# Attention and quantised FFN on one core: weights of the last projection queued behind a row fetch, a fixed order of evacuation, cast and store, and gate tiles taken one by one

## The chip, the cores and the metric

The kernel runs on one core of a Trainium2 chip. A core has a matrix engine (TensorE, PE in the profile, with its weight loads shown apart as PEld), a vector engine (VectorE, DVE), an activation engine (ScalarE, ACT), GpSimd (POOL) and a sync engine (SyncE, SP). In this kernel SP issues nearly all transfers between the chip's main memory and the on-chip buffers; POOL issues a few. Each engine works through its own list of instructions in order, and semaphores make one engine wait for another or for a transfer. The metric is the device time of one execution in microseconds. A smaller number is better.

## The reference

`x` is 2 batches x 2048 rows x 512 features in float32. Two blocks with residuals are computed:

```python
def xattn(h, ctx):                       # ctx: 128 rows per batch
    q = h @ Wq;  k, v = split(ctx @ Wkv)
    return softmax(q @ k.T / sqrt(512)) @ v

def ffn(x):                              # 512 -> 1536 -> 512
    x    = act_qdq(x)                    # 16-bit: scale = max|x| over the WHOLE tensor / 32767
    up   = act_qdq(x @ w4(w_up).T)       # w4: 4-bit weights in blocks of 32
    gate = act_qdq(x @ w4(w_gate).T)
    sig  = round(sigmoid(gate) * 65536) / 65536
    gate = act_qdq(gate * sig)
    o    = act_qdq(gate * up)
    return o @ w4(w_down).T

x = x + xattn(layernorm(x), ctx)
x = x + ffn(layernorm(x))
```

What shapes the kernel is `act_qdq`: its scale is a maximum over the whole tensor. No row of a tensor can be rounded until all rows of it are known, so each of gate, up and down is a stage that must end before the next one can begin.

## The kernel before

**Stages.** Attention comes first (to 177 us). It leaves the normalised rows in `hT`. Then three FFN stages follow. The 4096 rows are 8 groups of 512 (`TG`), and the 1536 FFN features are 12 blocks of 128, taken as 3 tiles of 4 blocks (`NK` x `NQ`). Integers of 16 bits are split into parts[...] (`split_integers`, lines 229 to 239), so that each product takes 12 matmuls of 128x512: 8 for the sum `q` and 4 for the correction `e` (`project`, lines 512 to 521).

- *Gate* (177 to 457 us): per group and block the `project`, then ACT copies `q` (line 565) and DVE subtracts `e` (line 566). The result goes to memory as `gate_d`. Lines 531 to 538 make the integers `hi` and the first group's parts before it.
- *Up* (457 to 729 us), lines 688 to 742: 24 tiles (`order`, from the last group to group 0), each in two halves `c` = 0 to 47 of 24 matmuls. ACT empties `q` (line 712) and DVE subtracts `e` (line 713). The PSUM pools of `q` and `e` have two buffers of one half each (line 583), so PE can begin half c only when half c-2 has been emptied. On the side, `next_gelu` (lines 632 to 638) reads one gate tile back and has ACT make its integers, its sigmoid and the rounded sigmoid (lines 606 to 608, three passes over 128x2048); DVE then makes the product's integers `pi` (line 644). It is called at c = 0 (three times over c = 0 and 1) and then at each even c. `bound` (lines 650 to 654) keeps for each half the largest |u|·p in a column of `pumax`.
- *The hinge between up and down* (729 to 750 us): the scale of `o` needs the largest product |u|·p in rounded numbers. `fetch_best` (lines 659 to 677) finds for each partition the half with the largest bound, and POOL fetches those rows back from memory with two indirect transfers (line 670, from `up_d` and `p_d`). They are rounded (line 764) and multiplied (line 766), a maximum over the partitions is taken (line 771), and it is compared with a floor. A flag (line 897) is read by all engines (line 899), and a branch that is not taken here covers the case that the bound was not enough.
- *Down* (750 to 1021 us), lines 953 to 974: 32 units `m` of 128 rows. ACT rounds u to `ui` (`round_up`, line 816, for a tile of 256 rows), DVE multiplies it with p to `oi` (line 835) and splits it: `sa` (836), ACT's cast to part 0 (838), part 1 (839), part 2 (843). PE makes `first_sum` (24 matmuls into `yq`, line 851) and `second_sum` (12 into `ye`, line 859). `finish` (lines 862 to 869) has ACT evacuate `yq` (865), POOL add the residual (867), DVE add `ye` (868), and SP store the rows (869). The parts have two buffers, and `yq` and `ye` four each.

**Weights of down.** `load_down` (lines 679 to 685) loads 12 blocks with 3 parts each; a whole block is 768 KB, parts 0 and 1 of it are 512 KB, part 2 is 256 KB. Blocks 0 to 3 (`first_wd`) go into the parts buffer that group 1 leaves, at the start of group 0; blocks 4 to 7 (their parts 0 and 1) after tile 21 and blocks 8 to 11 after tile 22; the part 2 of blocks 4 to 11 after the last store of u:

```python
        in_order(stored, *load_down(range(NE, NF), slice(2, 3)))
```

**What sets the order.** A scheduler of the language lays out each engine's list from the program; `in_order` (lines 158 to 166) forces an order between named instructions, without a wait. SP's transfers are issued in the order of its list and take turns on eight semaphores, so that each waits for the landing of the one eight before it.

Of the kernel before, what the change touches and what calls it, by code (L numbers as in the profile page):

```python
# [49 lines left out]
F32 = mybir.dt.float32  # L50
# [3 lines left out]
I16 = mybir.dt.int16  # L54
# [22 lines left out]
def tile_xattn_ffn(  # L77
# [167 lines left out]
    with ExitStack() as c0:  # L245
# [277 lines left out]
        with ExitStack() as c2:  # L523
# [6 lines left out]
            for c in range(ND):  # L530
                nc.vector.tensor_scalar(hi[:, c, :TG], hT[:, c, :TG], r_h, QMAX, ALU.mult, ALU.min)
            first = split_integers(wk1, homes[0], hi[:, :, :TG], [ND, TG], "g0", ND)
            for t in range(1, NG):
                if t % 2:
                    nc.vector.tensor_scalar(hi[:, :, ts(t, TG)], hT[:, :, ts(t, TG)], r_h, QMAX, ALU.mult, ALU.min)
                else:
                    nc.scalar.activation(hi[:, :, ts(t, TG)], hT[:, :, ts(t, TG)], AF.Copy, scale=r_h)
# [41 lines left out]
    with ExitStack() as c3:  # L579
# [108 lines left out]
        for j, (t, k) in enumerate(order):  # L688
            if k == 0:
                parts = groups.pop(t)  # L690
                if t + 1 < NG and t > 0:
                    groups[t - 1] = load_group(t - 1)
                if t == 0:
                    first_wd = homes[1].tile([P, 3, ND, TG], F32R, tag="parts", name="first_wd")
                    first_wd = first_wd.rearrange("p s c (k d) -> p (s c k d)", k=1).rearrange(
                        "p (f s d) -> p f s d", f=NE, s=3
                    )
                    load_down(range(NE))
            u4 = keep.tile([P, NQ, TG], F32, tag="u4", name=f"u4_{j}")
# [3 lines left out]
            for h in range(2):  # L703
# [22 lines left out]
                if c == 0:  # L726
                    pi = integers_of_p(0)
                if c < 2:
                    next_gelu()
# [8 lines left out]
            else:  # L738
                abs_max(umax[:, j : j + 1], u4[:, :2, :], AX.XY)
            if t == 0 and k + 1 < NK:  # L740
                load_down(range(NE + NQ * k, NE + NQ * (k + 1)), slice(0, 2))
        in_order(stored, *load_down(range(NE, NF), slice(2, 3)))

# [30 lines left out]
    with ExitStack() as c5:  # L774
# [4 lines left out]

        NS = TG // TD  # L780
        groups = [0, *reversed(range(1, NG))]

# [29 lines left out]

        def round_up(t, tiles, places=()):
            ui = wki.tile([P, NF, TD], I16, tag="ui5", name=f"ui5_{t}")
            for k in range(NK):
                made = nc.scalar.activation(  # L816
                    ui[:, ts(k, NQ), :], tiles[k][:, :, ts(t % NS, TD)], AF.Copy, scale=r_u
                )
                in_order(*places[k : k + 1], made)
            return ui  # L820

# [10 lines left out]
        def round_o(parts, pi, ui, c=slice(None)):  # L832
# [4 lines left out]
            ]  # L837
            nc.scalar.copy(parts[0][:, c], sa[:, c])  # L838
            made.append(nc.vector.scalar_tensor_tensor(parts[1][:, c], sa[:, c], -BASE, oi[:, c], ALU.mult, ALU.add))  # L839
            return made  # L840

# [19 lines left out]

        def finish(t, j, q, e, x1):
            m = t * (TD // P) + j
            qs = wk2.tile([P, D], F32, tag="qs", name=f"yqs_{m}")
            nc.scalar.activation(qs, q, AF.Copy, scale=q_o)  # L865
            qx = wk2.tile([P, D], F32, tag="qx", name=f"qx_{m}")
            nc.gpsimd.tensor_tensor(qx, qs, x1[:, j, :], ALU.add)  # L867
            nc.vector.scalar_tensor_tensor(qx, e, e_o, qx, ALU.mult, ALU.add)  # L868
            nc.sync.dma_start(out=of[ds(groups[t // NS] * TG + t % NS * TD + j * P, P), :], in_=qx)

# [18 lines left out]
        tiles_u, kept_p = kept_u[-NK:], kept_p[-NK:]  # L889

        uis = {0: round_up(0, tiles_u, rounded)}
        scale_of_pu()
# [56 lines left out]
        ld = c5.enter_context(tc.tile_pool(name="ld", bufs=2))  # L949
        units = range(TD // P)  # L950
        pieces = [ts(k, NQ) for k in range(NK)]
        p5, x1s = {}, {0: load_x1(0)}
        for t in range(NT // TD):
            if t + 1 < NT // TD:
                x1s[t + 1] = load_x1(t + 1)
                if t + 1 >= NS:
                    p5[t + 1] = load_p(t + 1)
            ui, x1 = uis.pop(t), x1s.pop(t)
            for j in units:
                m, w = t * len(units) + j, ts(j, P)  # L960
                parts = o_parts[m % 2]
                if t < NS:
                    at = ds(t * TD + j * P, P)
                    made = [round_o(parts, kept_p[k][:, :, at], ui[:, c, w], c) for k, c in enumerate(pieces)]
                    in_order(*chain(*made), *[third_part(parts, c) for c in pieces])
                else:
                    round_o(parts, p5[t][:, :, w], ui[:, :, w])
                    third_part(parts)
                q, e = first_sum(m, parts), second_sum(m, parts)
                if j == 0 and t + 1 < NT // TD:  # L970
                    uis[t + 1] = round_up(t + 1, tiles_u)
                    if t % NS == NS - 2 and t + NS < NT // TD:
                        tiles_u = load_up(groups[t // NS + 1])
                finish(t, j, q, e, x1)

# [22 lines left out]
```

## Time and profile before

Three runs took 1026.8, 1028.59 and 1028.76 us; the median is 1028.59 us. The profiled execution took 1027.3 us, of which 1025.5 us are the span from the first to the last instruction.

| stage | from, us | to, us | what the profile has there |
| --- | --- | --- | --- |
| attention, weights of gate | 0 | 177.5 | PE often idle |
| gate | 177.5 | 456.4 | PE without a gap |
| up | 457.3 | 729.1 | PE idle 3.6 us at 478.0 and 0.9 us at 491.7 |
| hinge | 729.1 | 750.2 | PE idle, but for one transpose of 0.29 us |
| down | 750.2 | 1021.4 | PE without a gap over 0.2 us |
| end | 1021.4 | 1025.5 | last addition and store |

Over the span PE is busy for 956.5 us (93%), DVE for 805.1, ACT for 546.5, POOL for 70.2. A line of the timeline gives start and duration in us, engine, source line, operation, output `<-` inputs, shapes, how many (`x`), and in brackets the engine's idle time before it with what ended it. A line of the waits gives who waited for whom, the sum in us, how often, and the longest. The busy digits of the page are tenths of 40 equal slices of 25.6 us.

### The profile page before, as it was taken

How to read it: one execution, taken by the hardware profiler on the slowest of the kernel's cores; microseconds unless marked ns; L12 is line 12 of the kernel's file. 1: busy time of each engine (PE TensorE's matmuls, PEld its weight loads, DVE VectorE, ACT ScalarE, POOL GpSimd, SP SyncE). 2: the span in 40 equal slices, each digit the busy share in tenths (PEclk: the TensorE clock that was granted, in tenths of full speed). 3: DMA queues.
4: the chain of work that ended last, by engine and by line, in shares of the span. 5: the costliest groups of instructions: out<-in, count | busy, mean ns of one | idle time of the engine just before them, and what ended most of it. 6: DMA issues, size and time to landing. Idle time of an engine off the chain costs nothing. (4 is left out here: it accounts for less than half of the span.)

```text
span 1025.5 us, 11691 instructions
## 1 busy us (share of the span) xinstructions
PE 956.5 (93%) x4321; PEld 762.0 (74%) x4321; DVE 805.1 (79%) x996; ACT 546.5 (53%) x647; POOL 70.2 (7%) x67
## 2 busy tenths in 40 slices
PE   6997875999999999998999999999479999999998
PEld 5765743788888878876788888888357888887776
DVE  4579865999997989445898987887589877777775
ACT  2268787332333323219998897887265343434332
POOL 0101111000000000000000000000011211111111
PEclk9999896999999999999999999999879999999999
DMA  9087644887895765896888987896957655754621
GB/s 338 32 313 268 238 186 175 337 334 274 309 384 183 300 226 174 272 395 264 329 326 351 367 318 298 321 387 255 380 210 238 201 151 207 237 201 136 225 84 62
DMA packets 103020, 263.72 MB, mean 257 GB/s; under 512 B 6000, under 2 KB 45936, under 8 KB 94256
## 3 DMA queue, kind: packets, MB, share of 16 engines
q1 hardware_dynamic: 101920, 259.02, 68.8%
q0 software_dynamic: 512, 2.88, 0.8%
q10 hardware_dynamic: 528, 1.05, 0.3%
q8 instruction: 34, 0.56, 0.2%
q14 instruction: 26, 0.21, 0.1%
HBM read 136.05 MB, written 126.88 MB: 256 GB/s over the span
## 5 line engine op out<-in xcount | busy, mean ns | idle before, releaser
L517 PE MATMUL q_g<-parts_g,wg 128*128 128x512 f32 x768 | 195.8, 395 | 5.0 <-ACT parts_g L236 5.0
L517 PEld LDWEIGHTS q_g<-parts_g,wg 128*128 128x128 f32 x768 | 143.5, 188 | 39.0 <-ACT parts_g L236 6.2
L565 ACT ACTIVATE g<-q_g 128x512 f32<-128x512 f32 x96 | 57.3, 599 | 183.0 <-PE q_g L517 176.5
L517 PE MATMUL q_u<-parts_u,wu 128*128 128x512 f32 x576 | 144.2, 392 | 0.0
L517 PEld LDWEIGHTS q_u<-parts_u,wu 128*128 128x128 f32 x576 | 107.9, 187 | 24.6
L851 PE MATMUL yq<-wd,o_parts 128*128 128x512 f32 x512 | 122.2, 391 | 0.0
L851 PEld LDWEIGHTS yq<-wd,o_parts 128*128 128x128 f32 x512 | 96.4, 188 | 21.3
L521 PE MATMUL e_g<-parts_g,wg 128*128 128x512 f32 x384 | 106.1, 395 | 0.0
L566 DVE CUSTOM_DVE_ANT_0 g<-g,e_g 128x512 f32<-128x512 f32 x96 | 64.6, 679 | 38.8 <-PE e_g L521 38.3
L838 ACT CAST o_parts<-sa 128x1536 fp32r<-128x1536 int16 (+1 forms) x40 | 48.6, 1215 | 85.0 <-DVE sa L836 85.0
L816 ACT ACTIVATE ui<-u,r_u 128x1024 int16<-128x1024 f32 x48 | 53.3, 1142 | 68.2 <-DVE oi L835 66.5
L851 PE MATMUL yq<-first_wd,o_parts 128*128 128x512 f32 x256 | 68.7, 410 | 19.5 <-ACT o_parts L838 19.5
L521 PEld LDWEIGHTS e_g<-parts_g,wg 128*128 128x128 f32 x384 | 71.9, 188 | 15.9
L521 PE MATMUL e_u<-parts_u,wu 128*128 128x512 f32 x288 | 77.9, 391 | 0.0
L851 PEld LDWEIGHTS yq<-first_wd,o_parts 128*128 128x128 f32 x256 | 47.9, 192 | 35.6 <-ACT o_parts L838 24.4
L653 DVE CUSTOM_DVE_ANT_0 ua<-ua,pi 128x1024 f32<-128x1024 f32 x47 | 57.4, 1221 | 20.8 <-ACT ua L652 20.6
L644 DVE SCALAR_TENSOR_TENSOR pi<-gi,k_p,sq 128x2048 int16<-128x2048 int16 x24 | 56.3, 2350 | 16.2 <-ACT sq L608 16.2
L713 DVE TENSOR_TENSOR u<-u,e_u 128x1024 f32<-128x1024 f32 x47 | 57.0, 1216 | 8.9 <-ACT u L712 8.8
L859 PE MATMUL ye<-wd,o_parts 128*128 128x512 f32 x256 | 63.9, 391 | 0.0
L521 PEld LDWEIGHTS e_u<-parts_u,wu 128*128 128x128 f32 x288 | 54.0, 187 | 12.3
L868 DVE SCALAR_TENSOR_TENSOR qx<-ye,e_o,qx 128x512 f32<-128x512 f32 x32 | 24.0, 749 | 47.8 <-POOL qx L867 43.3
L839 DVE SCALAR_TENSOR_TENSOR o_parts<-sa,oi 128x1536 fp32r<-128x1536 int16 (+1 forms) x40 | 57.5, 1439 | 3.6 <-DVE sa L836 0.5
(184 smaller groups left out, 1547.5 us busy)
## 6 DMA issues: line engine op xcount, KB each, us to landing
gate_d<-g SPq DMA_DIRECT2D x24, 1024.0 KB, 6.6
up_d<-u SPq DMA_DIRECT2D x48, 512.0 KB, 6.5
gt<-gate_d SPq DMA_DIRECT2D x22, 1024.0 KB, 8.4
u<-up_d SPq DMA_DIRECT2D x21, 1024.0 KB, 8.6
parts_d<-parts_g SPq DMA_DIRECT2D x6, 3072.0 KB, 11.2
parts_u<-parts_d SPq DMA_DIRECT2D x6, 3072.0 KB, 12.2
p_d<-pi SPq DMA_DIRECT2D x24, 512.0 KB, 10.2
p<-p_d SPq DMA_DIRECT2D x84, 128.0 KB, 3.0
```

Source lines behind the costliest of these rows:

```text
L517: nc.tensor.matmul(q, lhsT=w[:, s, c, :], rhs=parts[:, s, c, :], start=(c + s == 0), stop=(c + s == ND))
L521: nc.tensor.matmul(e, lhsT=w[:, 2, c, :], rhs=parts[:, 2, c, :], start=(c == 0), stop=(c == ND - 1))
L565: nc.scalar.activation(g4[:, i, :], q, AF.Copy, scale=1.0 + 1.0 / BASE)
L566: nc.vector.tensor_tensor_reduce(g4[:, i, :], g4[:, i, :], e, 1.0, LOWEST, ALU.subtract, ALU.max, gtop[:, m : m + 1])
L644: nc.vector.scalar_tensor_tensor(pi, gi, k_p, sq, ALU.mult, ALU.mult)
L653: nc.vector.tensor_tensor_reduce(ua, ua, pi, 1.0, 0.0, ALU.mult, ALU.max, pumax[:, c : c + 1])
L713: nc.vector.tensor_tensor(u4[:, both, :], u4[:, both, :], e, ALU.subtract)
L816: made = nc.scalar.activation(ui[:, ts(k, NQ), :], tiles[k][:, :, ts(t % NS, TD)], AF.Copy, scale=r_u)
L838: nc.scalar.copy(parts[0][:, c], sa[:, c])
L839: made.append(nc.vector.scalar_tensor_tensor(parts[1][:, c], sa[:, c], -BASE, oi[:, c], ALU.mult, ALU.add))
L851: nc.tensor.matmul(q, lhsT=parts[s][:, f, :], rhs=wd[f][:, s, :], start=(f + s == 0), stop=(f + s == NF))
L859: nc.tensor.matmul(e, lhsT=parts[2][:, f, :], rhs=wd[f][:, 2, :], start=(f == 0), stop=(f == NF - 1))
```

## The change

1. *Table.* A sigmoid of one column is put at the start of gate, on ACT, so that the load of the sigmoid's table stands there and no longer in front of the first sigmoid of up.
2. *Gate tiles.* `next_gelu` is called once at c = 0, once at c = 1, once at each even c from 2, and once more at c = 13. Before, c = 0 and 1 had three calls.
3. *Weights of down.* Blocks 0 to 3 come without their part 2 at first. Blocks 4 to 7, parts 0 and 1, come after tile 21 as before. The part 2 of blocks 0 to 3 comes after tile 22, where blocks 8 to 11 stood. Blocks 8 to 11 (parts 0 and 1) and the part 2 of blocks 4 to 11, twelve loads of 4 MB in all, come after the last store of u; before, these were eight loads of 2 MB.
4. *Down.* For group 0, `ui` is rounded for one unit of 128 rows at a time. The first unit's first tile is cut in two pieces. `finish` becomes `finish_first` (evacuation by ACT and addition by POOL) and `finish` (addition of `ye` by DVE and store), both two units later. Forced orders: on ACT the evacuation of unit m-2 before the first cast of unit m, and the rounding of the next u after the last cast of m; on DVE the addition of unit m-2 after the last part of m.

```diff
             first = split_integers(wk1, homes[0], hi[:, :, :TG], [ND, TG], "g0", ND)
+            table = const.tile([P, 1], F32, name="table")
+            nc.scalar.activation(table, unit, AF.Sigmoid)
...
-                    load_down(range(NE))
+                    load_down(range(NE), slice(0, 2))
...
-                if c < 2:
+                if c in (1, NH // 4 + 1):
                     next_gelu()
...
-            if t == 0 and k + 1 < NK:
-                load_down(range(NE + NQ * k, NE + NQ * (k + 1)), slice(0, 2))
-        in_order(stored, *load_down(range(NE, NF), slice(2, 3)))
+            if t == 0 and k == 0:
+                load_down(range(NE, NE + NQ), slice(0, 2))
+            if t == 0 and k == 1:
+                load_down(range(NE), slice(2, 3))
+
+        rest = load_down(range(NE + NQ, NF), slice(0, 2)) + load_down(range(NE, NF), slice(2, 3))
+        in_order(stored, *rest)
...
+        def round_up(ui, tiles, t, at=0, width=TD):
+            return [
+                nc.scalar.activation(
+                    ui[:, ts(k, NQ), ds(at, width)],
+                    tiles[k][:, :, ds(t % NS * TD + at, width)],
+                    AF.Copy,
+                    scale=r_u,
+                )
+                for k in range(NK)
+            ]
...
+        def finish_first(m, q, x1):
             qs = wk2.tile([P, D], F32, tag="qs", name=f"yqs_{m}")
-            nc.scalar.activation(qs, q, AF.Copy, scale=q_o)
+            made = nc.scalar.activation(qs, q, AF.Copy, scale=q_o)
             qx = wk2.tile([P, D], F32, tag="qx", name=f"qx_{m}")
-            nc.gpsimd.tensor_tensor(qx, qs, x1[:, j, :], ALU.add)
-            nc.vector.scalar_tensor_tensor(qx, e, e_o, qx, ALU.mult, ALU.add)
+            nc.gpsimd.tensor_tensor(qx, qs, x1[:, m % NU, :], ALU.add)
+            return made, qx
+
+        def finish(m, qx, e):
+            made = nc.vector.scalar_tensor_tensor(qx, e, e_o, qx, ALU.mult, ALU.add)
...
-        uis = {0: round_up(0, tiles_u, rounded)}
+        uis = {0: up_integers(0)}
+        in_order(rounded[0], *round_up(uis[0], tiles_u, 0, 0, P))
...
+        for m in range((last + 1) * NU + 2):
+            if m - 2 in sums:
+                q, e = sums.pop(m - 2)
+                t = (m - 2) // NU
+                evacuated, qx = finish_first(m - 2, q, x1s[t])
...
+                    sizes = [2, 2, NQ, NQ] if m == 0 else [NQ] * NK
...
+                if m > 1:
+                    in_order(evacuated, casts[0])
+                sums[m] = first_sum(m, parts), second_sum(m, parts)
+                if m + 1 < NS * NU:
+                    t, j = divmod(m + 1, NU)
+                    if j == 0:
+                        uis[t] = up_integers(t)
+                    in_order(casts[-1], *round_up(uis[t], tiles_u, t, j * P, P))
+                    if m + 2 == NS * NU:
+                        tiles_u = load_up(groups[1])
+                elif t < last and j == (NU - 1 if t + 1 == NS else 0):
+                    uis[t + 1] = up_integers(t + 1)
+                    in_order(casts[-1], *round_up(uis[t + 1], tiles_u, t + 1))
...
+            if m > 1:
+                stored = finish(m - 2, qx, e)
+                if m - 2 < last * NU + NU - 2:
+                    in_order(made[-1], stored)
```

## The prediction

> **What bounds the kernel.** I read the page first, its busy slices, to see where PE is not full.
>
> ```profile
> PE   6997875999999999998999999999479999999998
> PEclk9999896999999999999999999999879999999999
> ```
>
> From slice 7 on PE is full but for slice 18 (461 to 487 us) and slices 28 and 29 (718 to 769). Matmuls are not changed, so time can come only from there. The waits of PE in 440 to 720 us and from 720 on name the two places:
>
> ```profile
> PE q_u L517 <- ACT u L712: 4.6, 2, 3.6
> PE yq L851 <- ACT o_parts L838: 19.5, 5, 18.8
> ```
>
> The timeline at the start of up shows the first:
>
> ```profile
> 464.82 3.90 ACT L606 ACTIVATE gi<-gt,r_g 128x2048 int16<-128x2048 f32 x2 [0.63 <-DMA wu<-wu_d]
> 468.62 3.88 ACT L607 ACTIVATE gt<-gi,s_g 128x2048 f32<-128x2048 int16 x2
> 472.41 3.69 ACT L608 ACTIVATE sq<-gt 128x2048 uint16<-128x2048 f32 x2
> 476.95 1.91 ACT L712 ACTIVATE u<-q_u 128x1024 f32<-128x1024 f32 x2
> 478.01 5.10 PE L517 MATMUL q_u<-parts_g,wu 128*128 128x512 f32 x15 [3.62 <-ACT u L712]
> ```
>
> Two gate tiles go through ACT in pairs, 11.5 us, ahead of the evacuation of half 1 that PE needs for half 3. The next windows show what the stall also costs: the granted clock is 0.50 in 478 to 481 us, so 3.0 us of matmuls do 1.5 us of work.
>
> The timeline of the hinge shows the second:
>
> ```profile
> 725.04 5.40 SPq L723 DMA_DIRECT2D up_d<-u  x2
> ...
> 728.01 0.16 DVE L665 SCALAR_TENSOR_TENSOR row<-where,lane 128x1 uint32<-128x1 uint32 x1
> ...
> 730.50 6.02 SPq L684 DMA_DIRECT2D wd<-wd_d  x8
> ...
> 736.21 1.07 POOL L670 DMA_INDIRECT best<-up_d,row  x1 [275.90 <-DMA wd<-wd_d]
> ...
> 742.72 1.15 ACT L764 ACTIVATE ui_b<-best,r_u 128x1024 int16<-128x1024 f32 x1 [9.30 <-DMA best<-up_d,row]
> ...
> 745.17 4.49 ACT L816 ACTIVATE ui<-u,r_u 128x1024 int16<-128x1024 f32 x4 [1.30 <-DVE two L766]
> ...
> 747.86 0.75 DVE L835 SCALAR_TENSOR_TENSOR oi<-pi,k_o,ui 128x512 int16<-128x512 int16 x1 [1.17 <-DVEq L900]
> ...
> 749.57 0.60 ACT L838 CAST o_parts<-sa 128x512 fp32r<-128x512 int16 x1
> ...
> 750.22 3.78 PE L851 MATMUL yq<-first_wd,o_parts 128*128 128x512 f32 x8 [18.76 <-ACT o_parts L838]
> ```
>
> The row is known at 728.17, yet POOL fetches only at 736.21. The fetch reads `up_d`, so it needs the store of half 46, issued at 725.04; that one transfer took 10.2 us to land by the trace (735.3), and POOL starts 0.9 later. The page gives 6.5 us as this kind of store's median. The windows say why it is slow: the DMA share is 0.98 to 1.05 in every stretch from 705 to 740. About 400 GB/s move without a pause, and the store stands behind `wd` loads.
>
> [...] the fetch landed after 6.5 us while SP's eight loads were under way. [...]
>
> **The change part by part.**
>
> *Table.* 1.28 us leave ACT at 461.6 and come, with about 0.3 us of sigmoid, in front of an `hi` of 2.0 us and the group's casts 3 and 4, which end at 180.94 and would end near 182.5. By the built order, PE then has four matmuls of block 1, and further corrections, ahead of those casts' matmuls: twelve matmuls by about 182.0, the other twelve of the two blocks at 0.23 us each from 182.1, about 185.0. Before, block 1 ends at 185.2 (the last four start at 184.13). I take 0. At worst the whole 1.6 us shows; it cannot gain.
>
> *Gate tiles.* Replay ACT in its built order with the rows' durations: maxima from 461.3 (0.8 without the table), u of half 0 to 463.3, gi 1.98, `ua` 1.05, sigmoid 1.98, then u of half 1 from 468.4 to 469.4. PE arrives at half 3 at 474.4, five us later. Next sq 1.88, gi, `ua`, sigmoid, u of half 2 to 477.3; PE arrives at half 4 at 479.8. Both stalls go: 3.62 + 0.93 + the 1.5 of the clock = 6.1 us. What is late next: ACT has 2x1.0 (u) + 2x1.05 (`ua`) + 1.98 + 1.98 + 1.88 = 9.9 us per tile against 11.1 us of PE. The added call at c = 13 puts 5.8 us into a slack of 1.2 per tile, so about five tiles run with evacuations late; half-deep buffers cover most of it, and following the list I find some 1 us of PE waits between halves 13 and 24. Gain 5, between 3 (stalls of 3 there) and 6.1. Gate tile loads need no earlier landing: two are on chip at 463.5, and SP's issues are only spread out.
>
> *Weights of down.* Ahead of the store of half 46 stand 1 MB of part 2 less (four loads of 512 KB, not 768) and then 1 MB where 2 MB stood. At 410 KB per us that is 2 MB / 0.41 = 5 us. The backlog is then gone by about 728.5, and the store lands by 729.4 (5.9 earlier; the floor is 2.6 us, which the lightly loaded store at 693.46 needed, or 727.7, but the row is not ready before 728.2). Fetch at 730.0 for 736.2: 6.2 us gained, between 5 and 7.2. The price: SP now issues twelve loads from 730.5, each 0.5 to 0.75 us and never over eight in flight, to about 739. Queued behind them on SP are the flag and the x1 loads, not needed before the flag at 740. Their 4 MB need 10 us, to about 742, beside the fetch. The fetch had 2 MB in flight beside it before, so its 6.5 us may stay; I allow 0 to 2 more and take 0.5. Block 8 is wanted six us after PE's start and lands by 735; part 2 is wanted later still. All of this is relative to PE's end of up, so it adds to the other gain.
>
> *First unit of down.* From DVE's first `oi` to PE's first matmul: 2.36 us (747.86 to 750.22), as four roundings of 1.14 hold ACT until 749.66. In the changed order three half-size roundings (about 0.6 each) stand there, and the first piece has 256 elements, not 512: 0.4 + 0.2 + 0.35 + 0.3 for signals = 1.25. Gain 1.1. The next pieces come at 1.05 and 1.75 us; PE, at half clock for its first 3.8 us, takes 1.9 per piece, so it does not run dry.
>
> *Order in down.* From 750 to 1021 PE has four gaps of 0.17 to 0.19 us: at most 0.7 to gain. Per unit DVE needs 1.82 + 0.56 + 1.76 + 1.75 + 0.75 = 6.6 us and ACT 1.47 + 0.68 + 1.5x1.14 = 3.9, in PE's 8.44. The evacuation of m-2 is old when the cast of m comes, so the forced order waits for nothing. The tight place is unit 4. By the built order its cast follows the evacuation of unit 3, which ends its first sum 2.77 us before unit 4 begins: 0.68 + 1.47 = 2.15 leaves 0.6, if `ui` is there. Its u loads are now issued after x1 (that waits for POOL's addition of unit 1) and land near 29 us after PE's start; `ui` ends at 30.2, `sa` at 32.7, the cast at 35.3, PE wants it at 35.8. I take +0.7 to -1.5, and 0.4 gained.
>
> *Sum.* 0 + 5.0 + 6.2 - 0.5 + 1.1 + 0.4 = 12.2 us. The profiled execution goes from 1027.3 (span 1025.5) to 1015.1. The median lies 1.3 above that execution, so 1016.4.
>
> **Rivals.** (A) The fetch is not sooner: POOL starts at 730, but 4 MB of SP's loads hold it until their end near 742, plus 2. The attribution "DMA wd" in POOL's line speaks for a tie to the loads; the 6.5 us beside a full queue speaks against. Then the hinge gains only 0.1, and 5 + 0.1 + 0.4 leave about 1023. (B) The stall moves: with only one tile of lead ACT falls behind, and up loses at halves 13 to 24 what it won at 3 to 5. For it: ACT is busy 175 of the 200 us from 500 to 700. Then 7.2 are left: about 1021. (C) Slower: in down the three roundings of the next `ui` (3.4 us) come to stand between an evacuation and the next cast. After a first sum's end 2.77 us are left, 0.68 + 3.42 + 1.47 = 5.6 are needed: 2.8 us per 256 rows, fourteen times, 39 us: about 1055. It decides from 0.9 us per 256 rows, where 12.2 are eaten. Against it: the built order has evacuation, cast, evacuation, cast, and only then the roundings.
>
> **How the numbers follow.** A difference of 0.2% (2 us) is what a measurement of this kernel can tell. Likeliest, with its own range of 1012.5 to 1019: 0.62. (A) 0.13, (B) 0.13, both at once, near 1028, 0.05, (C) 0.07. Faster 0.62 + 0.13 + 0.13 = 0.88, same 0.05, slower 0.07. From 1011.5 to 1022.5 the range holds the likeliest, most of (B) and half of (A): 0.8.
>
> **What would show it.** Right: no wait of PE for u over 1 us near 478 and clock 1.00 there; POOL's fetch within 2 us of the row, about 6 us after half 46's store is issued or sooner; PE idle for about 13 us, not 19, before its first `yq`; 36 matmuls per 8.44 us after that. Wrong: ACT of the fetched u more than 8 us after POOL's start (A); PE waits for u past 520 us (B); PE waits for casts in every second unit, or at unit 4 (C); a wait at 180 us (table). The forecast fails if the backlog ahead of half 46 is set by something other than the 2 MB removed.

## The result, and the profile after

The changed kernel takes 1022.36 us (median of five runs, 1020.75 to 1023.37) where the kernel before takes 1028.67 (five runs beside it). The ratio is 0.9932, with a 95% interval of 0.9913 to 0.995. The gain is 6.3 us: about half of the 12.2 that were forecast. It lies just inside the whole range given (1011.5 to 1022.5 us), and outside the range that the likeliest outcome had for itself (1012.5 to 1019). Where it was made and lost is quite different from the forecast, and that is the subject of what follows.

The busy slices of the changed kernel's page, from the same rows as before:

```profile
PE   6998874999999999999999999999488999999998
PEclk9999997999999999999999999999789999999999
```

The dip at slice 18 (461 to 487 us) is gone from the row of PE; the row of the clock has a 9 there before and after. The dip of the hinge (slices 28 and 29) is still there, and slice 30 has a small new one in the row of PE. The waits of PE, for 440 to 720 us and for 720 us on (who waited for whom, sum in us, times, longest), say the same:

```profile
PE q_u L517 <- ACT u L715: 0.3, 1, 0.3
...
PE yq L865 <- ACT o_parts L854: 20.4, 2, 17.1
```

The wait of up has fallen from 4.6 us to 0.3. The wait for `o_parts` was 19.5 with a longest of 18.8. It is now larger in sum, with a longest of 17.1: there is a second one, of 3.23 us, inside down. The timeline at the start of up and in the hinge:

```profile
463.92 2.00 ACT L609 ACTIVATE gi<-gt,r_g 128x2048 int16<-128x2048 f32 x1 [0.99 <-DMA wu<-wu_d]
...
468.67 1.00 ACT L715 ACTIVATE u<-q_u 128x1024 f32<-128x1024 f32 x1
...
476.70 2.03 PE L517 MATMUL q_u<-parts_g,wu 128*128 128x512 f32 x8
...
720.62 4.18 SPq L726 DMA_DIRECT2D up_d<-u  x2
...
723.08 0.16 DVE L668 SCALAR_TENSOR_TENSOR row<-where,lane 128x1 uint32<-128x1 uint32 x1
...
724.90 10.40 SPq L687 DMA_DIRECT2D wd<-wd_d  x12
...
729.99 1.07 POOL L673 DMA_INDIRECT best<-up_d,row  x1 [270.09 <-DMA wd<-wd_d]
...
737.00 1.15 ACT L772 ACTIVATE ui_b<-best,r_u 128x1024 int16<-128x1024 f32 x1 [8.75 <-DMA best<-up_d,row]
...
743.43 3.78 PE L865 MATMUL yq<-first_wd,o_parts 128*128 128x512 f32 x8 [17.14 <-ACT o_parts L854]
```

One gate tile, not two, stands ahead of the evacuation at 468.67, and no matmul waits. In the hinge the row is known at 723.24 but POOL fetches at 729.99, 6.75 us later. Before, it was 8.04. The store of half 46, issued at 720.62, needed 8.4 us to land by the trace (before: 10.2). That is the step where the forecast had expected 6.2 us and got about one.

The new wait in down, at the fifth unit of 128 rows (unit 4), in the timeline of the changed kernel:

```profile
764.80 1.60 SPq L801 DMA_DIRECT2D u<-up_d  x3
...
775.12 1.15 ACT L828 ACTIVATE ui<-u,r_u 128x1024 int16<-128x1024 f32 x1 [1.04 <-DMA u<-up_d]
...
775.91 4.02 POOL L880 TENSOR_TENSOR qx<-yqs,x 128x512 f32<-128x512 f32 x2 [14.41 <-DMA out<-qx]
...
776.31 2.51 DVE L850 SCALAR_TENSOR_TENSOR oi<-p,k_o,ui 128x1536 int16<-128x1536 int16 x1 [1.76 <-ACT ui L828]
...
778.85 1.50 DVE L851 TENSOR_SCALAR sa<-oi 128x1536 int16<-128x1536 int16 x1
...
781.96 3.60 PE L865 MATMUL yq<-first_wd,o_parts 128*128 128x512 f32 x8 [3.23 <-ACT o_parts L854]
```

ACT waits for the third of the three loads of u. DVE then needs 2.51 and 1.50 us for two operations that took 1.82 and 0.56 in the kernel before, while POOL makes two additions. PE stands for 3.23 us, and the granted clock is 0.50 for the next 3.4 us.

The two profiled executions, stage by stage (times from the first and last matmul of each stage):

| stage | before, us | after, us | gained |
| --- | --- | --- | --- |
| up to the first matmul of up | 457.32 | 456.92 | 0.4 |
| up | 271.73 | 266.60 | 5.1 |
| hinge: PE's last `q_u` or `e_u` to its first `yq` | 21.18 | 19.91 | 1.3 |
| down | 271.19 | 272.11 | -0.9 |
| end | 4.12 | 3.87 | 0.2 |
| span | 1025.5 | 1019.4 | 6.1 |

The 0.4 us of the first row are no gain of the change: in the other kernels below, up begins between 456.1 and 458.6 us.

### The profile page after: what moved, and what is told of

It is laid out like the page before. It is cut to its first block, busy times and chain, and to the rows that moved or that the text cites. A ratio compares the mean times of both kernels' runs of the same rounds, so it can differ in the third digit from the quotient of the medians.

```text
span 1019.4 us, 11685 instructions
## 1 busy us (share of the span) xinstructions
PE 953.6 (94%) x4321; PEld 764.6 (75%) x4321; DVE 806.2 (79%) x1000; ACT 549.4 (54%) x655; POOL 90.4 (9%) x67
## 3 DMA queue, kind: packets, MB, share of 16 engines
q0 software_dynamic: 512, 2.88, 0.7%
q10 hardware_dynamic: 528, 1.05, 0.3%
## 5 line engine op out<-in xcount | busy, mean ns | idle before, releaser
L865 PEld LDWEIGHTS yq<-wd,o_parts 128*128 128x128 f32 x512 | 96.6, 189 | 21.1
L865 PE MATMUL yq<-first_wd,o_parts 128*128 128x512 f32 x256 | 68.3, 411 | 20.4 <-ACT o_parts L854 20.4
L878 ACT ACTIVATE yqs<-yq,q_o 128x512 f32<-128x512 f32 x32 | 22.0, 687 | 119.1 <-PE yq L865 119.1
L880 POOL TENSOR_TENSOR qx<-yqs,x 128x512 f32<-128x512 f32 x32 | 64.5, 2016 | 210.6 <-ACT yqs L878 152.0
L865 PEld LDWEIGHTS yq<-first_wd,o_parts 128*128 128x128 f32 x256 | 50.1, 196 | 32.7 <-ACT o_parts L854 21.0
L857 DVE SCALAR_TENSOR_TENSOR o_parts<-sa,oi 128x1536 fp32r<-128x1536 int16 (+2 forms) x41 | 58.2, 1438 | 19.9 <-PE ye L873 19.9
L656 DVE CUSTOM_DVE_ANT_0 ua<-ua,pi 128x1024 f32<-128x1024 f32 x47 | 57.1, 1220 | 18.8 <-ACT ua L655 18.6
L853 DVE SCALAR_TENSOR_TENSOR o_parts<-sa,oi 128x1536 fp32r<-128x1536 int16 (+2 forms) x41 | 58.6, 1430 | 14.9 <-PE yq L865 13.0
L854 ACT CAST o_parts<-sa 128x1536 fp32r<-128x1536 int16 (+2 forms) x41 | 48.8, 1190 | 34.4 <-DVE sa L851 34.4
## 6 DMA issues: line engine op xcount, KB each, us to landing
parts_d<-parts_g SPq DMA_DIRECT2D x6, 3072.0 KB, 11.1
```

What stands on the lines that cost most here:

```text
L656: nc.vector.tensor_tensor_reduce(ua, ua, pi, 1.0, 0.0, ALU.mult, ALU.max, pumax[:, c : c + 1])
L857: return nc.vector.scalar_tensor_tensor(parts[2][:, c], sa[:, c], BASE + 1.0, oi[:, c], ALU.mult, ALU.subtract)
L865: nc.tensor.matmul(q, lhsT=parts[s][:, f, :], rhs=wd[f][:, s, :], start=(f + s == 0), stop=(f + s == NF))
L880: nc.gpsimd.tensor_tensor(qx, qs, x1[:, m % NU, :], ALU.add)
```

## The experiments

Three questions came out of this comparison, and the theories carry these names in the expectations:

- *Where did the gain of the hinge go?* T1: the gate-tile edit leaves ACT's last gate tiles later relative to PE, the store of half 43 comes late, and the weight loads that SP has queued behind it restore the backlog. T2: the backlog ahead of half 46 never depended on the 2 MB. T4: the fetch itself is slowed by the loads that run beside it. T5: its duration is its own.
- *What makes the wait at unit 4?* T3: the late loads of u. Its rival: the collision of POOL and DVE.
- *What is the forced order in down worth?* T6: the order is what counts. T7: it is enough that the evacuations and additions come two units later.

All times below are medians. Ratios are to the kernel before, run on the same chip beside them. The stage figures are of each kernel's profiled execution.

| kernel | time, us | ratio, 95% interval | up | fetch issued / p rows landed, after PE's end of up | hinge | units 3 and 4 together | twelve units 19 to 30 |
| --- | --- | --- | --- | --- | --- | --- | --- |
| before | 1028.67 | | 271.7 | 7.2 / 14.3 | 21.2 | 17.0 | 103.0 |
| changed | 1022.36 | 0.9932 (0.9913 to 0.995) | 266.6 | 6.5 / 14.5 | 19.9 | 21.5 | 99.4 |
| gate tiles alone | 1021.22 | 0.9925 (0.9907 to 0.9943) | 266.4 | 6.0 / 13.7 | 20.7 | 16.6 | 102.9 |
| weights of down alone | 1027.41 | 0.9992 (0.9982 to 1.0002) | 272.4 | 3.6 / 13.0 | 21.6 | 16.6 | 101.9 |
| down alone | 1029.29 | 1.0007 (0.9998 to 1.0016) | 272.7 | 7.3 / 14.6 | 20.4 | 22.4 | 99.4 |
| changed, old gate tiles | 1027.48 | 0.9996 (0.9985 to 1.0006) | 273.1 | 3.7 / 12.7 | 18.2 | 22.4 | 99.4 |
| changed, no early table | 1018.81 | 0.9909 (0.9895 to 0.9924) | 266.2 | 2.6 / 12.0 | 17.4 | 24.2 | 99.4 |
| changed, loads ahead of the store | 1020.51 | 0.9917 (0.9901 to 0.9933) | 269.2 | 1.9 / 11.4 | 16.8 | 23.9 | 99.4 |
| changed, rest behind the flag | 1023.28 | 0.9945 (0.9932 to 0.9958) | 268.4 | 6.1 / 11.8 | 17.2 | 24.6 | 99.4 |
| changed, tile rounded whole | 1018.47 | 0.9901 (0.9889 to 0.9914) | 267.2 | 6.3 / 14.4 | 19.8 | 18.1 | 99.4 |
| changed, three qx buffers | 1022.77 | 0.9942 (0.9929 to 0.9955) | 267.2 | 5.9 / 14.6 | 20.0 | 21.1 | 99.4 |
| changed, two orders not forced | 1021.96 | 0.9943 (0.9929 to 0.9956) | 266.6 | 5.6 / 14.4 | 19.7 | 20.9 | 99.4 |
| loads ahead + rounded whole | 1018.19 | 0.9904 (0.9888 to 0.992) | 267.8 | 2.0 / 11.8 | 17.2 | 17.6 | 99.4 |
| the same + part 2 behind the flag | 1017.04 | 0.99 (0.9884 to 0.9915) | 266.6 | 1.8 / 11.1 | 16.5 | 17.9 | 99.4 |

A unit is counted from its first `yq` matmul to that of the next unit, so that the wait of PE for unit 4 falls into unit 3, and the slow clock after it into unit 4.

How far a stage differs by itself can be read from four of these kernels that are alike up to down: the changed one, and those with the tile rounded whole, with three qx buffers and with two orders not forced. Their up is 266.6 to 267.2 us, their fetch is issued 5.6 to 6.5 us after PE's end of up, and their hinge is 19.7 to 20.0.

### The edits one by one

**Gate tiles alone**, in the kernel before:

```diff
-                if c < 2:
+                if c in (1, NH // 4 + 1):
```

> The gate-tile calls alone, in the kernel before. Both theories: up from its first matmul to its last is about 5 us shorter (271.7 before, 266.6 in the changed kernel), since both stalls of PE near 478 and 491 us go. For the hinge (PE's last matmul of up to its first of down, 21.2 us before) they differ. T1 (the last gate tiles come later relative to PE, and with them the store of half 43 and the weight loads queued behind it): the hinge gets longer by 1 to 4 us, and the kernel gains 1 to 4 us in all. T2 (the backlog of transfers ahead of half 46 does not hang on this): the hinge stays at 21.2 and the kernel gains 5 us, about 1023.5.

Up falls by 5.4 us, as both theories said. But the hinge does not get longer; at 20.7 it is 0.5 shorter. T1 in this form falls: this edit by itself delays nothing. It is also faster, by its median, than the whole change. The intervals overlap, so I only say that the other edits together brought nothing that can be measured. The kernel with the old gate tiles, below, says the same from the other side.

**Weights of down alone**, in the kernel before (the third part of the change, nothing else):

```diff
-                    load_down(range(NE))
+                    load_down(range(NE), slice(0, 2))
...
-        in_order(stored, *load_down(range(NE, NF), slice(2, 3)))
+        rest = load_down(range(NE + NQ, NF), slice(0, 2)) + load_down(range(NE, NF), slice(2, 3))
+        in_order(stored, *rest)
```

> The new placing of down's weights alone, in the kernel before. Up stays at 271.7 us. T1 (the gate-tile edit ate the gain of this one): with the gate tiles where they were, the store of half 46 lands within 4 us and the fetch is issued 4 to 6 us earlier relative to PE's end of up than before (7.2 us after it): hinge 15.5 to 17 us instead of 21.2, about 1023.5. T2 (the backlog never hung on the 2 MB that the edit moves away): hinge 20 to 21 us, about 1028.

Neither theory is right. The fetch is issued 3.5 us earlier, so the backlog does hang on the 2 MB (against T2), though not by 5. The fetch then takes 8.3 us to land where it took 6.5, and what is left is lost in the next step. The timeline of this kernel, between the fetch and PE's start:

```profile
742.87 6.34 ACT L820 ACTIVATE ui<-u,r_u 128x1024 int16<-128x1024 f32 x6 [1.33 <-DVE two L770]
...
749.39 1.66 ACT L842 CAST o_parts<-sa 128x512 fp32r<-128x512 int16 x3 [0.17 <-ACTq L904]
```

The scheduler has put six roundings of u in ACT's list ahead of the first cast. The kernel before had four there. An edit of SP's loads has moved ACT's list.

**Down alone**, in the kernel before: everything of the fourth part of the change.

> The new order of down alone, in the kernel before. The hinge is about 1.1 us shorter (first piece of half size). Then T3: a stall of PE of 3 to 5 us at the fifth unit of 128 rows, with its lost clock, is paid, and the last twelve units run at 8.28 us each instead of 8.60, which returns about 4: about 1.5 us in all faster, 1027. If the stall hung on the other edits instead, it is absent here and the gain is 5 to 6 us, 1023.

T3's account holds in its parts. The hinge is 0.8 shorter. The stall at unit 4 is there without the other edits: a wait of 4.1 us, and units 3 and 4 cost 5.4 us more. The late units run at 8.28 us and return 3.6. The first unit takes 0.9 longer. The time was expected at 1027 and came out at 1029.3: within the interval, this edit alone gains nothing.

**The changed kernel with the old gate tiles** (`c < 2` again):

> The changed kernel with the gate-tile calls of the kernel before. Up is 5 us longer, 271.7. T1: the hinge is 4 to 5 us shorter than in the changed kernel (19.9), 15 to 16 us, so the time stays within 1 us of 1022.4. T2: the hinge stays at 19.9 us and the time is 5 us longer, about 1027.4.

The time is 1027.48, as T2 had it. The ratio of 0.9996 has an interval that holds 1: without the gate tiles the three other edits together gain nothing that can be measured. The hinge lies in between: 18.2, not 15 to 16 and not 19.9. Of these 1.7 us, 1.6 are lost again in down (273.8 us instead of 272.1). Compared with down alone (20.4), which differs by the weights and the early table, the placing of the weights is worth 2.15 us here: the fetch is issued 3.6 earlier and takes 8.1 instead of 6.7.

**The changed kernel without the early table:**

```diff
-            table = const.tile([P, 1], F32, name="table")
-            nc.scalar.activation(table, unit, AF.Sigmoid)
```

> The changed kernel without the early sigmoid. If the prediction's nothing for this edit holds: within 1 us of 1022.4. In detail: the load of 1.28 us stands ahead of the first sigmoid of up again, so that ACT's list in the first five halves is 1.3 us later; a delay of 2.2 us there (a late landing of the first gate tile, in another execution) gave a wait of PE of 1.5 us near half 5, so 0.6 us of wait are expected here, and 0 to 0.4 come back at the start of gate: plus 0.5.

I expected half a microsecond more. By the ratios the time fell by about 2.4 us (0.9909 against 0.9932), but the intervals overlap. The trace has the key to the hinge, which is 17.4 us instead of 19.9. The wait near half 5 is there as expected (0.62 us). The cause of the shorter hinge is 20 us ahead of it. ACT's list in the changed kernel, in the timeline, with SP behind it:

```profile
705.06 1.00 ACT L715 ACTIVATE u<-q_u 128x1024 f32<-128x1024 f32 x1
...
709.12 2.21 SPq L687 DMA_DIRECT2D wd<-wd_d  x4
```

and in the kernel without the table:

```profile
702.13 1.03 ACT L713 ACTIVATE u<-q_u 128x1024 f32<-128x1024 f32 x1 [0.42 <-PE q_u L517]
...
704.87 2.28 SPq L685 DMA_DIRECT2D wd<-wd_d  x4
...
727.32 1.07 POOL L671 DMA_INDIRECT best<-up_d,row  x1 [265.78 <-DVE m_u L752]
```

Both first lines are the evacuation of half 43. Without the table it stands ahead of the last gate tile's sigmoid and runs as soon as PE is done. With the table the scheduler has laid the list so that the sigmoid, an absolute value and the rounded sigmoid come first. The store behind it is issued 20.3 us before PE's end of up without the table and 14.8 before it in the changed kernel, 5.5 later. SP works through its list in order, and the four loads of blocks 4 to 7 stand behind that store (issued at 708.70 in the changed kernel). In the changed kernel PE had freed their buffers at 701.5, yet they were issued from 709.12 on, and the DMA share meanwhile (a window of the trace: start:end, length, busy times by engine, clock, DMA share, GB/s) was

```profile
704.00:707.00 3.00, 3.00 (x15) 2.49 (x14) 2.43 (x3) 2.83 (x3) 0.00 (x0) 1.00 0.00 1
```

nothing at all. Two megabytes that could have moved then stood in front of half 46's store later. ACT's list in up is the same in this kernel as in the one with the gate tiles alone, so the difference is the table's. It takes both edits, though: with the old gate tiles, ACT's list in up is that of the kernel before, table or not. T1's chain (late evacuation, late store, loads held behind it, restored backlog) was right; the gate tiles by themselves did not start it.

That these 2.5 us reach the time is not shown. The profiled execution of this kernel was the slowest of its five (1022.9 us; the others 1017.5 to 1020.7). In it units 3 and 4 took 24.2 us instead of 21.5, and hinge and down together 292.5 instead of 292.0.

### The chain of the hinge, taken at two other links

**Loads of blocks 4 to 7 ahead of half 43's store:**

```diff
+                if c == NH - 5:
+                    load_down(range(NE, NE + NQ), slice(0, 2))
                 stored = nc.sync.dma_start(out=up_d[c], in_=u4[:, both, :])
...
-            if t == 0 and k == 0:
-                load_down(range(NE, NE + NQ), slice(0, 2))
```

> The changed kernel, but the loads of blocks 4 to 7 stand on SP ahead of the store of half 43 (which came late from ACT) and no longer behind it. T1 (this queueing gave the fetch's gain away): the loads are issued near 702 instead of 709 us, the pause of the transfers from 705 to 709 is filled, and the fetch is issued 2.5 to 4 us after PE's end of up, where the changed kernel has 6.5 and the one with the old gate tiles 3.7. As the fetch then takes about 8 us beside 4 MB of loads, it lands some 2 earlier and the hinge is 18 us instead of 19.9: about 1020.5. If the late store of half 43 is not the cause: fetch at 6.5, hinge 19.9, 1022.4.

The evacuation is as late as in the changed kernel, but the loads no longer wait for it. The timeline of this kernel:

```profile
703.74 2.20 SPq L687 DMA_DIRECT2D wd<-wd_d  x4
...
727.67 1.07 POOL L673 DMA_INDIRECT best<-up_d,row  x1 [268.16 <-DVE umax L169]
```

The fetch is issued 1.9 us after PE's end of up and the hinge is 16.8, 3.1 less than in the changed kernel. That shows the link from SP's order to the hinge. The time, 1020.5, is as expected, with an interval that overlaps that of the changed kernel. The hinge gave more than the 1.9 us expected, but in the profiled execution up had a wait of 1.5 us near 487 (the first gate tile landed 2.2 us later), and units 3 and 4 cost 2.4 us more.

**The twelve last loads behind the flag:**

```diff
-        rest = load_down(range(NE + NQ, NF), slice(0, 2)) + load_down(range(NE, NF), slice(2, 3))
-        in_order(stored, *rest)
...
         p5, x1s = {}, {0: load_x1(0)}
+        rest = load_down(range(NE + NQ, NF), slice(0, 2)) + load_down(range(NE, NF), slice(2, 3))
+        in_order(x1_loads[0], *rest)
```

> The changed kernel, but the twelve loads of 4 MB that stood behind the last store of u are issued only behind the flag and the first x1 load, so that no load runs beside the fetch. T4 (the fetch is slow because of the loads that run beside it): POOL's fetch is issued at the same point, about 6.5 us after PE's end of up, and lands within 3.5 us instead of 7.0; the hinge is 16 to 16.5 us instead of 19.9 and the time about 1018.5, unless PE then waits for block 8 in its first sum. T5 (6.5 to 7 us are what this fetch costs by itself): the fetch still takes 6.5, the hinge stays within 0.5 us, 1022.

The timeline of this kernel, fetch and first use:

```profile
731.23 1.08 POOL L673 DMA_INDIRECT best<-up_d,row  x1 [271.52 <-DVE two L772]
...
735.65 1.15 ACT L770 ACTIVATE ui_b<-best,r_u 128x1024 int16<-128x1024 f32 x1 [5.81 <-DMA best<-up_d,row]
```

4.4 us from issue to landing with nothing beside it (the 3.5 of the expectation was an estimate), against 7.0 in the changed kernel and 8.1 to 8.3 where the fetch is issued early beside the 4 MB. T4 holds, T5 falls. The hinge is 2.7 us shorter, about what the fetch saved. The gain did not reach the time, which is 1023.3 and not 1018.5. In the profiled execution the first two units, whose matmuls are interleaved on PE in this kernel, took 0.9 us more together, and units 3 and 4 took 3.1 us more, with a wait of PE at unit 4 that grew to 5.1 us.

### Unit 4

**The second tile of group 0 rounded whole**, one unit earlier than its second half would be, so that its buffers come free for the next u:

```diff
-                if m + 1 < NS * NU:
+                if m + 2 < NS * NU:
...
-                    in_order(casts[-1], *round_up(uis[t], tiles_u, t, j * P, P))
-                    if m + 2 == NS * NU:
+                    in_order(casts[-1], *(round_up(uis[t], tiles_u, t, j * P, P) if t == 0 else round_up(uis[t], tiles_u, t)))
+                    if m + 3 == NS * NU:
```

> The changed kernel, but the second tile of group 0 is rounded whole after the first unit's casts of down's unit 1, so that the next group's u is loaded one unit earlier. T3 (the stall at unit 4 comes from the u loads, which wait for the last rounding in halves): the loads are issued near 759 instead of 764.8 us and land by 770; the wait of PE of 3.2 us at unit 4 falls below 0.5, the clock is not halved there, and the time is 4 to 5 us shorter, about 1018. If the collision of POOL's additions with DVE makes the stall, a wait of 1.5 us or more stays, and the gain is 1 to 2.

The timeline of this kernel:

```profile
757.09 2.45 SPq L801 DMA_DIRECT2D u<-up_d  x3
...
776.14 1.82 DVE L850 SCALAR_TENSOR_TENSOR oi<-p,k_o,ui 128x1536 int16<-128x1536 int16 x1 [0.55 <-ACT ui L828]
...
780.17 2.22 PE L865 MATMUL yq<-first_wd,o_parts 128*128 128x512 f32 x8 [1.18 <-ACT o_parts L854]
```

The loads are issued 7.7 us earlier and have all landed by 767.6. The wait of PE is 1.18 us, not below 0.5, but the clock stays at 1.00, and units 3 and 4 cost 18.1 us instead of 21.5. The time is 1018.5, 3.2 us below the changed kernel by the ratios, whose intervals overlap by 0.0001. T3 holds for most of the stall.

The wait at unit 4 also decides what a shorter hinge is worth. It stands in the changed kernel and in six variants of it: old gate tiles, no early table, loads ahead of the store, rest behind the flag, three qx buffers, two orders not forced. In the profiled executions of these seven the hinge goes from 20.0 down to 16.8 us, yet hinge and down together take 291.6 to 293.3 in all of them. The third u lands 50.0 to 51.8 us after PE's end of up, whether down began early or late, so what the hinge saves is mostly spent at unit 4. Why the landing hardly moves was not tried.

**Three buffers for qx:**

```diff
-            qx = wk2.tile([P, D], F32, tag="qx", name=f"qx_{m}")
+            qx = wk2.tile([P, D], F32, tag="qx", name=f"qx_{m}", bufs=3)
```

> The changed kernel with three buffers for qx instead of two: POOL's addition of unit 2 no longer waits for the store of unit 0, which lands late behind the 3 MB of u loads. The multiplication and the split of unit 4 on DVE (2.51 and 1.50 us while POOL adds) fall back to 1.82 and 0.56, the cast comes 1.6 us earlier, and PE's wait at unit 4 falls from 3.2 to about 1.6: 1.5 to 2 us faster than the changed kernel, 1020.6. If POOL's additions do not slow DVE, both durations stay and so does the time.

The multiplication fell back to 1.82 us, but the split did not. The timeline of this kernel at unit 4:

```profile
778.68 2.33 POOL L880 TENSOR_TENSOR qx<-yqs,x 128x512 f32<-128x512 f32 x1 [4.82 <-ACT yqs L878]
...
779.91 1.52 DVE L851 TENSOR_SCALAR sa<-oi 128x1536 int16<-128x1536 int16 x1
```

POOL's addition of unit 2 now waits for its evacuation, which ACT makes only after the late roundings (777.93). So it still falls on unit 4. PE's wait went from 3.23 to 2.60, and the time did not change. The part of the collision that went was worth 0.6 us of PE's wait, and the split still takes 1.0 us more than its 0.56. The collision is itself a consequence of the late u, and a buffer does not remove it.

### The forced order in down

```diff
-                if m > 1:
-                    in_order(evacuated, casts[0])
...
-                stored = finish(m - 2, qx, e)
-                if m - 2 < last * NU + NU - 2:
-                    in_order(made[-1], stored)
+                finish(m - 2, qx, e)
```

> The changed kernel without two of its forced orders in down (evacuation of unit m-2 ahead of the first cast of unit m, addition of unit m-2 behind the last part of unit m); the evacuations and additions still come two units later. T6 (the forced order is what keeps DVE from waiting for POOL's addition in the late units): the unit of 128 rows takes 8.5 us or more again in the last third, and the time is 2 to 4 us longer than the changed kernel, 1024.5 to 1026.5. T7 (coming two units later is enough, the forced order does nothing): the late units stay at 8.28 us, and the time is within 1 us of 1022.4.

The scheduler then puts the cast of unit m ahead of the evacuation of unit m-2 and the addition ahead of the next multiplication, but the late units stay at 8.28 us and the time at 1022. T7 holds and T6 falls. What made the late units slow in the kernel before is in its window of eight of them (start:end, length, busy times of PE, PEld, DVE, ACT and POOL, clock, DMA share, GB/s):

```profile
936.00:1005.00 69.00, 68.47 (x290) 53.52 (x290) 52.44 (x40) 25.86 (x25) 10.39 (x9) 1.00 0.43 142
```

and in its waits of DVE over the same stretch:

```profile
DVE qx L868 <- POOL qx L867: 14.1, 8, 2.0
```

52.4 us of work and 14.1 of waiting for POOL leave DVE 2.5 of 69: there DVE, not PE, sets 8.6 us per unit. PE's weight loads show it: in this stretch they waited 3.4 us for ACT's cast of what DVE had split. In the kernel without the two orders the same wait, over its stretch of eight units, is

```profile
DVE qx L884 <- POOL qx L880: 10.7, 9, 1.2
```

still there, but at most 1.2 us each and inside PE's 8.28. In the changed kernel it is gone from this stretch, and DVE waits for PE. The addition comes two units later, and POOL has mostly done its part.

### Both cures together

Loads ahead of the store and the tile rounded whole:

> The loads of blocks 4 to 7 ahead of the store of half 43 and the second tile of group 0 rounded whole, both in the changed kernel. If the two causes are separate, their gains add: hinge 16.8 us instead of 19.9 (3.1) and a stall at unit 4 of 1.2 us without the loss of the clock (3.3): about 1016. If the earlier start of down only makes PE wait longer at unit 4 (the u loads hang on ACT, whose roundings start when down starts, so it should not): 1018 to 1019.

The same, with the part 2 of blocks 4 to 11 behind the flag:

> As the kernel with both edits, and the part 2 of blocks 4 to 11 (eight loads, 2 MB) is loaded only behind the flag and the first x1 load; blocks 8 to 11, parts 0 and 1, stay ahead of the fetch. T4 says that the fetch takes 8.2 us beside 4 MB and 4.4 beside none, so about 6.5 beside 2 MB: hinge 15 to 15.5 us instead of 16.8, and 1014.5. Part 2 is first wanted some 7 us after PE's start of down and lands about 8 us after the flag; if it comes late, PE waits for it in the first unit and the gain is lost: 1016 or more.

In the traces the gains add: hinge plus down is 286.1 and 285.4 us, against 292.0 in the changed kernel and 288.6 with the tile rounded whole alone. In the times they hardly do: 1018.2 and 1017.0, where 1016 and 1014.5 were expected, with intervals that hold 0.9901, the ratio of the rounded tile alone. That the hinge's 2.5 us reach the time is therefore seen in the trace and not shown by the clock. The last expectation's estimate of the fetch was wrong: beside 2 MB it takes 8.0 us, as beside 4 MB. PE does not wait for part 2. The last kernel has the lowest median of all, 1.0% below the kernel before (0.99, interval 0.9884 to 0.9915). Its interval and that of the changed kernel (0.9913 to 0.995) overlap by 0.0002. It cannot be told apart from the kernel with only the tile rounded whole.

## Why the prediction was right in total and wrong in its parts

The total was right by luck. The forecast was 6.0 us too low, and the measured time is 0.14 us inside the end of a range that had been drawn wide enough for most of (B) and half of (A). It is a time that the prediction gave to these rivals, though (B) did not happen and (A) only in part. By experiment the whole gain, as far as it can be measured, is that of the gate tiles: 0.9925 with them alone, 0.9996 with everything but them. What the weights were to bring did not come, and the gain and the loss in down nearly cancelled. Of the signs that the prediction named for being right, only the one at 478 us and the pace of the units came true. The fetch came 6.75 us after the row and not within 2, PE stood 19.9 us before its first `yq` and not 13, and it waited at unit 4, which had been named as a sign of being wrong.

- **Table: 0 predicted.** The load of the sigmoid's table takes 1.28 us in both traces, at 461.60 in the kernel before (`461.60 1.28 ACT L607 ACT_TABLE_LOAD   x1`) and at 177.25 in the changed one. The prediction is right at the edit's own place: from the first matmul of gate to that of up, all executions here took 279.8 to 280.9 us, with the table or without it. Wrong elsewhere: together with the gate tiles it cost 2.5 us of hinge. I looked for its price where the instruction stands and not at what else the scheduler had laid differently, though ACT's list of up, which the prediction replays for its first halves, has half 43 behind the last sigmoid.
- **Gate tiles: 5.0.** Measured 5.1 in the changed kernel and 5.4 alone. The expected microsecond of waits in halves 13 to 24 was one wait of 0.3. With it the prediction's own terms give 5.8 (6.1 less 0.3); the other 0.7 is not accounted for, and up differs by 0.6 between kernels that are alike there. Rival (B) is out.
- **Weights of down: 6.2 less 0.5.** Beside the old gate tiles and with the new down, 2.15 us of hinge (18.2 against 20.4); in the kernel before and in the changed kernel, nothing. The first failing step is "the backlog is then gone by about 728.5": 2 MB at 410 KB per us should have moved the landing of half 46's store by 5 us, and it moved by 3.5 where nothing else interfered (6.2 to 2.7 us after PE's end). The "About 400 GB/s move without a pause" behind it holds from 715 us on; from 705 to 710 the same windows have 369, and from 710 to 715 they have 333. The trace shows where the time went: with the old gate tiles the store of half 43 lands 3.1 us sooner, but from there to the landing of the last of the next four loads, 2 MB, it takes 7.5 us instead of 5.1. Why it does is open. The second failing step is "I take 0.5" for the slower fetch: it was 1.5 (6.7 to 8.1). So rival (A) was partly true: the loads slow the fetch but do not hold it to their end (in the changed kernel it landed at 736.98 us and the last of them at 742.08). The third is the table. The fourth is "so it adds to the other gain": while the wait at unit 4 stood, what was won in the hinge was lost there. The condition I had named as fatal, that something other than the 2 MB sets the backlog, came true: SP's order behind a late store.
- **First unit of down: 1.1.** Right. From the first `oi` to PE's first matmul it took 1.29 us (742.14 to 743.43) instead of 2.36. That is nearly all of the 1.3 us that the hinge gained. The 0.3 us for signals in the sum were an estimate; the trace has 0.04, 0.08 and 0.06 between the four instructions. The half clock of PE's first 3.8 us is in the windows of both: the granted clock is 0.50 from 733.6 to 754.0 us in the kernel before and from 727.2 to 747.6 in the changed one, and 1.00 behind it.
- **Order in down: 0.4, from +0.7 to -1.5.** The net in down was -0.9, inside that range, but as the difference of two terms that were both missed. The gain in the late units, 3.6 us, was held to at most 0.7, because I counted PE's four visible gaps (0.7 us) and not the pace of the units, which rose from 8.28 to 8.6 without gaps. The loss at unit 4 was about 4.6 us: the third u landed 31.7 us after PE's start and not 29, and the 1.82 and 0.56 us of DVE were taken from a row in which POOL was not adding at that moment. The waits of the kernel before had the sign of the first: DVE waited 43.3 us for POOL's additions from 720 on.

The kernel before shows the collision of POOL and DVE, early in down:

```profile
757.46 0.29 DVE L836 TENSOR_SCALAR sa<-oi 128x512 int16<-128x512 int16 x1
...
759.09 1.29 POOL L867 TENSOR_TENSOR qx<-yqs,x 128x512 f32<-128x512 f32 x1 [13.48 <-ACT yqs L865]
...
759.25 1.28 DVE L836 TENSOR_SCALAR sa<-oi 128x512 int16<-128x512 int16 x1
```

A split of 128x512 took 0.29 us alone and 1.28 when it started 0.16 us after an addition of POOL of 1.29. In the changed kernel it took 1.38 when it started 0.06 us after one (760.27). At 798.76 there, DVE's multiplication started 0.07 us ahead of an addition: it kept its 1.80 us, and the addition took 2.88. What makes the two engines hold each other up, no run here shows. The prediction should have priced it.

## What to carry to other kernels

Where a scheduler lays the lists, cost an edit by every list that it changes, not only at its own line: beside the new gate tiles, an instruction added at 177 us moved an evacuation at 702 us, and that was worth 2.5 us of the hinge. Look also at what stands behind the stage that you shorten: here, in the traces, a shorter hinge made PE wait longer at unit 4, until the u loads came sooner. On an in-order queue, look at what stands behind a store that waits for a late engine; loads whose buffers are free belong ahead of it (here the hinge was 16.8 us with them ahead and 19.9 with them behind). And read a loop's pace from the distance between its units, not from the gaps of the engine: a pace of 8.6 instead of 8.28 us showed no gap of PE worth the name.

## What the runs showed of the hardware

- An indirect fetch of 128 rows landed 4.4 us after its issue with nothing beside it, 6.5 to 7.6 where it was issued 5.6 to 7.3 us after PE's end of up, in the midst of a queue of loads, and 8.0 to 8.3 where it was issued 1.8 to 3.7 us after it, together with 2 or 4 MB of loads. An earlier issue was thus worth only a part of itself.
- From the landing of half 43's store to that of the last load of blocks 4 to 7 it took 5.1 us in the kernel before and 7.5 in the changed kernel with the old gate tiles, with a DMA share of 1.05 and 0.95 from 715 to 720 us (401 and 315 GB/s). What makes the difference was not tried.
- The wait of PE at unit 4 was 3.2 us in the changed kernel and 4.0 to 4.8 in the three that differ from it only ahead of down. In these the x load ahead of the u loads was issued 1 us later and the third u landed 33.2 to 33.6 us after PE's start instead of 31.7. Where this begins was not tried either. With the tile rounded whole it was 0.7 to 1.2.
- Each wait of PE at unit 4 of 2.5 us or more went with a stretch at a granted clock of 0.50, which began within 1.4 us of its end: 3.4 us long for waits of 2.5 to 4.1, 6.8 us long for waits of 4.3 to 5.1. After the waits of 0.7 to 1.2 the clock stayed at 1.00. The waits of 2.5 and 2.6 are those with two orders not forced and with three qx buffers. In up of the kernel before, the wait of 3.62 us that ended at 478.0 went with 3.4 us at 0.50 (477.6 to 481.0), and after the wait of 0.93 that ended at 491.7 the clock stayed at 1.00.
